# Two graph layers on one core: first weights behind the apply, and other places for biases, loads and norm parts

## The chip, the cores and the metric

The kernel runs on one core of a Trainium2 chip. A core has five engines, each with its own instruction stream: TensorE (PE, matrix multiplication, with weight loads as a second row PEld), VectorE (DVE), ScalarE (ACT), GpSimd (POOL) and SyncE (SP). SP, ACT and POOL also start DMA transfers, each through a queue of its own. Matmul results land in PSUM and are read from there by DVE or ACT.

The metric is the device time of one launch in microseconds. Six runs of the kernel before gave a median of 1492.16 us, between 1490.14 and 1496.52.

## The reference

`x` has 8 batches, 2048 nodes and 64 features; `adj` is a 2048 x 2048 matrix. Two layers follow each other. Both apply a polynomial of the graph, with weights of their own for each node, made from an embedding of 16 numbers per node:

```python
# layer 0: supports I, A, 2*A@A - I
w = einsum('nd,dkio->nkio', embedding, weight);  b = einsum('nd,do->no', embedding, bias)
out = einsum('bnki,nkio->bno', einsum('knm,bmc->bnkc', A_stack, x), w) + b
x = layernorm(x + out)
# layer 1: the same three supports of adj, and a fourth
apt = softmax(relu(E @ E.T), axis=1)
x = layernorm(x + out_of_four_supports)
```

## The kernel before

The nodes are cut into 8 blocks of 256 (`NBLK`, `NB`), two slabs of 128 each. There are 40 stages, 8 for each of five phases, numbered n = 8 * phase + j:

- A0: u = A x of layer 0, and for block j the part of the output that comes from x and u (stages 0 to 7)
- B0: A u, the third support, and the layer norm (8 to 15)
- A1: the same as A0 for layer 1, and row maxima and sums for the softmax (16 to 23)
- Z1: the softmax matrix times x (24 to 31)
- V1: A u for layer 1, the last weights, the norm and the output (32 to 39)

Each stage has one large product on PE (`straight`, `strassen`, `turned`). Most products are done by a Strassen scheme of seven products, named p1 to p7; a product goes to one of two PSUM accumulators (`ps_acc`, two buffers), and DVE or ACT adds it up elsewhere before that accumulator can be used again.

Between the matmuls of the product other work is put by hand: `put(n, i, f, ...)` says that `f` is emitted in stage n when i of 64 parts of its product are done; `spread` puts a list of jobs at even distances. So the order on each engine is written out in the lines 738 to 843, and all engines execute in that order. The jobs that matter here:

- `weights(g0, g1)` (line 313): makes groups of the weights of a block, `pw` = embedding times weight pool, four matmuls each, into a PSUM buffer of the pool `big` (three buffers); `copy` evicts it into `w`, on DVE (even first argument) or on ACT. The 16 groups of a block are cut into six bursts (`cuts`). `w_room` is one buffer: all weights of a block are used before those of the next are written.
- `apply(c)` (line 334): `po` = features times weights, 64 small matmuls in four calls; each call takes one `big` buffer, and DVE adds it to `acc` in four instructions. In stages A0, A1 and V1 all four calls stand at one place (`bursts`).
- `bias` (line 301): `pb`, then two DVE additions into `bx`, which POOL stores in DRAM; `load_acc` reads it back as the first value of `acc`.
- `post(k)` (line 363): after the apply. With k = 0 it stores `acc` (A0, A1), or starts the norm: mean and squares (0), the sum of the squares and the root (1), the multiplication and the store (2).
- `load_e` loads the embedding of a block (`e2`, two buffers), and for Z1 the softmax constants `c`.
- `load_x` reads the normed x of a block back (`x1d`) as a slab of `X` for layer 1.
- `repeat(s)` (line 569): in B0 a half of the features `t` has to stand in both halves of the partitions, so it is copied by a DMA (`t<-t`).
- `wst` and `adj` (class `Ahead`): SP's loads of weight pools and adjacency tiles, a few tiles ahead.

The last B0 stage (j = 7) has its own places, since layer 1's first product, in stage 16, already reads x:

```python
bursts, posts = (6, 6, 12, 12), ()
put(n + 1, 26, st.load_x, range(SB))
for k in range(6):
    put(n + 1, (13 if k < 3 else 14) + 2 * k, st.post, k % 3, 8 - k // 3 * 8, 16 - k // 3 * 8)
```

Of the kernel before, what the change touches and what calls it, by code (L numbers as in the profile page):

```python
# [23 lines left out]
NBLK = N // NB  # L24
SB = NB // P
# [4 lines left out]
V1 = C // 4  # L30
# [18 lines left out]
def two_graph_layers(ctx: ExitStack, tc: tile.TileContext, x, x_t, adj_b, adj_q, layers, out):  # L49
# [21 lines left out]
    pe, dve, act, pool = (Pinned(tc, e) for e in (nc.tensor, nc.vector, nc.scalar, nc.gpsimd))  # L71
# [18 lines left out]
    def big(name):  # L90
        return ps_big.tile([P, 2, 512], F32, tag="big", name=name)

    def copy(i, dst, src):

        if i % 2:
            act.activation(dst, src, AF.Copy)
        else:
            dve.tensor_copy(dst, src)
# [42 lines left out]
    ps = big("pi")  # L141
# [120 lines left out]
    class Stage:  # L262
# [50 lines left out]
        def weights(self, g0, g1):  # L313
            if g0 == 0:
                self.w = w_room[:, 0:NB * self.units].rearrange("p (n o) -> p n o", n=NB)
            made = []
            for g in range(g0, g1):
                if g % 4 == 0:
                    self.ws = wst.next()
                ps = big("pw").rearrange("p h (v n) -> p h v n", n=NB)  # L320
                for i in range(2):
                    for h in range(2):
                        r = slice(64 * h, 64 * h + 64)
                        pe.matmul(ps[:, h, i, :], self.ws[r, 2 * (g % 4) + i, :], self.e2[r, :],
                                  start=True, stop=True)
                made.append(ps)
            if g1 == self.units // 4:
                wst.fill()
            for g, ps in zip(range(g0, g1), made):
                dst = self.w[:, :, 4 * g:4 * g + 4].rearrange("p n (v h) -> p n v h", h=2)  # L330
                copy(0 if g % (8 if self.phase == "A0" else 3) == 1 else 1, dst, ps.rearrange("p h v n -> p n v h"))


        def apply(self, c):
# [234 lines left out]
        def repeat(self, s):  # L569

            if self.wide:
                self.pair[s].store_z()
            if self.half:
                t = self.t[:, s * P:(s + 1) * P, :]
                pool.dma_start(out=t[64:128, :, :], in_=t[0:64, :, :])

        def turned(self, stationary, moving):

# [133 lines left out]
    sums = {}  # L712
# [27 lines left out]
    def put(n, i, f, *args):  # L740
        plans[n].setdefault(i * stages[n].length / 64, []).append((f, args))

    def spread(n, first, last, jobs):
        for i, job in enumerate(jobs):
            put(n, first + (last - first) * i / max(len(jobs) - 1, 1), *job)
# [20 lines left out]
        put(1, place, sums["A0"].make, i)  # L766
    put(8, 2, load_u, (NBLK - 1,))
    for i in range(4):
        put(16, 24 + 4 * i, sums["A1"].make, i, 0, 7)
        put(16, 50, sums["A1"].make, i, 7, 8)  # L770
    for i, place in ((0, 10), (2, 20), (3, 30)):
        put(32, place, sums["V1"].make, i)
# [1 line left out]
    for n, st in enumerate(stages):  # L774
        phase = st.phase
        cuts = (0, 3, 6, 9, 12, 14, 16) if st.units == C else (0, 3, 6, 8)
        weights = [(st.weights, *g) for g in zip(cuts, cuts[1:])]
        bursts = None
        if phase == "A0":
            for c in range(NJ // 4 if st.j == 1 else 0):  # L780
                put(n, 16 * c + 10, st.sums_of_a, c)
            spread(n + 1, 1, 31, weights)
            turned, bursts, posts = 33, (38, 38, 38, 38), (50,)
        elif phase == "B0":
            if st.j == 7:
                spread(n, 40, 60, weights)
                bursts, posts = (6, 6, 12, 12), ()
                put(n + 1, 26, st.load_x, range(SB))
                for k in range(6):
                    put(n + 1, (13 if k < 3 else 14) + 2 * k, st.post, k % 3, 8 - k // 3 * 8, 16 - k // 3 * 8)  # L790
            else:
                spread(n + 1, 3, 13, weights)
                bursts, posts = (19, 19, 29, 29), (38, 42, 48)
                put(n + 2, 5, st.load_x, range(SB))
        elif phase == "A1":
            spread(n + 1, 12, 36, weights)
            turned, bursts, posts = 4, (43, 43, 43, 43), (56,)
            for s, h, place in ((0, 0, 38), (0, 1, 40), (1, 0, 57), (1, 1, 60)):
                put(n, place, st.scores_of_rows, s, h)
            put(n, 41, st.statistics, 0)  # L800
            put(*((n, 62) if st.j else (n + 1, 6)), st.statistics, 1)
            put(n + 1, 24, st.store_c)
        elif phase == "V1":
            spread(n, (22 if st.j else 4), (62 if st.j < 7 else 52), weights)
            bursts, posts = (4, 4, 4, 4), (15, 19, 23)
            put(n, 20, st.load_z)
        if bursts and n + 1 < len(stages):
            if phase[0] == "A":
                put(n + 1, turned, st.turn, 1)
            for i, place in enumerate(bursts):  # L810
                put(n + 1, place, st.apply, i if phase == "A0" else i ^ 2)
            for k, place in enumerate(posts):
                put(n + 1, place, st.post, k)
        if n + 1 < len(stages):
            if n < 25 or n > 30:
                put(n, 44 if n < 23 else 37 if n < 25 else 4, stages[n + 1].load_e)
        if phase[0] == "A":
            put(*((1, 12) if n == 0 else (n, 28) if st.li == 0 else (n, 37)), st.bias)
            if st.li == 0:
                put(max(n, 1), 20 if n else 4, st.load_xt)  # L820
            else:
                put(n, 47 if st.j else 57, st.turn, 0, "x")
        if phase != "Z1":
            put(*((1, 26) if n == 0 else (n, 48 + 6 * st.li) if st.kk == 0 else (n, 30)), st.load_acc)
        elif st.wide:
            first, even, odd = (n - 2, (16, 24, 32), (40, 48, 56)) if n % 2 == 0 else (n - 2, (28, 36, 44), (4, 12, 20))
            load = (n - 2, 4) if n % 2 == 0 else (n - 3, 20)
            if n == 26:
                first, even, odd, load = 25, (4, 10, 18), (20, 26, 34), (24, 40)
            elif n == 27:  # L830
                first, even, odd, load = 25, (56, 61, 67), (42, 48, 54), (25, 33)
            put(*load, st.load_e)
            for t, places in enumerate((even, odd)):
                for i, place in enumerate(places):
                    at = (first, place) if place < 64 else (first + 1, place - 64)
                    put(*at, *((st.numerators, t, i) if i < 2 else (st.normalize, t)))
        else:
            st.p = [None] * 8
            for c in range(8):
                if c < 3:  # L840
                    put(n - 1, (50, 54, 62)[c] if n < 26 else 40 + 8 * c, st.scores, c)
                else:
                    put(n, 8 * (c - 3), st.scores, c)
# [71 lines left out]
```

## Time and profile before

| what | us |
|---|---|
| median of six runs | 1492.16 |
| the profiled execution | 1492.26 |
| its span on the core | 1490.5 |
| PE busy | 1452.7 |
| DVE busy | 954.1 |
| ACT busy | 473.8 |
| POOL busy | 206.7 |

The page cuts the span into 40 slices of 37 us. A digit is the busy share in tenths:

```profile
PE   9899999999999999899999999999999999999996
DVE  3876666637666666766666666568794466666665
ACT  1344444432211213064444444432110233333332
PEclk9999999999999999999999999999999999999998
DMA  9788898884666666578877887212313656666551
```

The first nine slices are A0, the next seven or so B0, then A1 from about 600 us, Z1 from about 930 us and V1 from about 1165 us to the end. PE is busy nearly always, so the engines beside it matter where PE waits for them. A PE that is busy is not a PE that works without loss: switches between kinds of matmuls, and a slower clock, count as busy.

The costliest groups of the page are these (busy us in total, mean ns of one, idle time before and what ended it):

```profile
L43 ACT ACTIVATE w<-pw 128x1024 f32<-128x1024 f32 x328 | 318.4, 1021 | 392.7 <-PE pw L43 388.1
L43 DVE SCALAR_TENSOR_TENSOR acc<-po,mask,acc 128x256 f32<-128x256 f32 (+1 forms) x640 | 247.0, 426 | 83.2 <-PE po L43 70.4
L43 DVE COPY w<-pw 128x1024 f32<-128x1024 f32 x120 | 146.9, 1224 | 141.7 <-PE pw L43 140.4
```

All operations go through one helper, so every line is L43, and one has to go by the names of the tiles.

### The profile page before, as it was taken

To read this page: it belongs to the slowest core of one execution; us is meant where nothing else is said; L and a number is where in the kernel's file an instruction comes from. 1 tells how busy PE (TensorE), PEld (TensorE's weight loads), DVE (VectorE), ACT (ScalarE), POOL (GpSimd) and SP (SyncE) were. 2 spreads that over 40 slices of the span, in tenths; PEclk is the share of its full clock that TensorE was granted. 3 is DMA by queue.
4 is the path that set the end of the run, shared out by engine and by line. 5 is a ranking of instruction groups with operands and counts; after the bars stand their busy time and mean duration, and the time that the engine had idled before them with its cause. 6 is when DMAs were issued, how large, how long until landed. Compare 5 with 4: busy or idle time off the path is not lost.

```text
span 1490.5 us, 31130 instructions
## 1 busy us (share of the span) xinstructions
PE 1452.7 (97%) x13310; PEld 1183.2 (79%) x13310; DVE 954.1 (64%) x1614; ACT 473.8 (32%) x590; POOL 206.7 (14%) x343
## 2 busy tenths in 40 slices
PE   9899999999999999899999999999999999999996
PEld 4467777778999999468777777788888888888885
DVE  3876666637666666766666666568794466666665
ACT  1344444432211213064444444432110233333332
POOL 4222221210111111111011111101100000000100
PEclk9999999999999999999999999999999999999998
DMA  9788898884666666578877887212313656666551
GB/s 361 250 281 263 276 280 266 271 314 156 203 191 200 203 203 206 146 172 183 201 195 169 207 210 207 52 40 65 91 43 115 203 180 194 190 190 192 192 192 54
DMA packets 86730, 283.37 MB, mean 190 GB/s; under 512 B 14016, under 2 KB 18112, under 8 KB 84992
## 3 DMA queue, kind: packets, MB, share of 16 engines
q1 hardware_dynamic: 53600, 171.99, 39.6%
q0 software_dynamic: 27520, 95.76, 21.0%
q10 hardware_dynamic: 5472, 13.63, 2.8%
q8 instruction: 105, 1.72, 0.5%
q14 instruction: 33, 0.27, 0.1%
HBM read 216.28 MB, written 60.83 MB: 186 GB/s over the span
## 4 chain that ended last, share of the span: by engine, by line
PE 70%; issue 20%; DVE 3%; DMA 3%; POOL 3%; ACT 1%; POOLq 0%; ACTq 0%; DVEq 0%
PE p L43 40%; PE po L43 11%; PE pw L43 8%; PE pz L43 6%; PE pu L43 2%; PE pt L43 1%; DMA x<-in_x 1%; DVE w L43 1%; PE pr L43 1%; DVE acc L43 1%; PE ps L43 1%; POOL e L43 1%; POOL x1d L43 1%; DMA u<-in_w 1%; DMA wst<-wd 1%
## 5 line engine op out<-in xcount | busy, mean ns | idle before, releaser
L43 ACT ACTIVATE w<-pw 128x1024 f32<-128x1024 f32 x328 | 318.4, 1021 | 392.7 <-PE pw L43 388.1
L43 DVE SCALAR_TENSOR_TENSOR acc<-po,mask,acc 128x256 f32<-128x256 f32 (+1 forms) x640 | 247.0, 426 | 83.2 <-PE po L43 70.4
L43 DVE COPY w<-pw 128x1024 f32<-128x1024 f32 x120 | 146.9, 1224 | 141.7 <-PE pw L43 140.4
L43 PE MATMUL p<-a,u 128*128 128x128 f32 x1792 | 219.7, 278 | 4.1 <-PE p L43 3.9
L43 PEld LDWEIGHTS p<-a,u 128*128 128x128 f32 x1792 | 206.7, 192 | 15.1 <-issue 5.0
L43 PE MATMUL po<-w,t 128*32 128x256 f32 (+1 forms) x5120 | 205.8, 337 | 6.0 <-issue 3.1
L43 PE MATMUL p<-u,a 128*128 128x256 f32 x832 | 203.6, 387 | 0.0
L43 PEld LDWEIGHTS po<-w,t 128*32 128x32 f32 (+1 forms) x5120 | 125.9, 108 | 79.6 <-issue 12.0
L43 PEld LDWEIGHTS p<-u,a 128*128 128x128 f32 x832 | 152.1, 190 | 29.7 <-issue 5.4
L43 PE MATMUL p<-x,a 128*128 128x256 f32 x624 | 152.6, 385 | 0.0
L43 PE MATMUL pw<-e,wst 64*128 64x256 f32 x1728 | 146.1, 297 | 1.6 <-ACT w L43 1.1
L43 PEld LDWEIGHTS pw<-e,wst 64*128 64x128 f32 x1728 | 112.2, 184 | 42.3 <-issue 21.5
L43 PEld LDWEIGHTS p<-x,a 128*128 128x128 f32 x624 | 114.3, 190 | 18.9 <-issue 0.7
L43 PE MATMUL pu<-x,a 128*128 128x512 f32 x192 | 91.9, 626 | 2.8 <-DMA x<-x1d 2.6
L43 PE MATMUL p<-w,u 128*128 128x256 f32 x384 | 85.8, 379 | 0.0
L43 PE MATMUL p<-a,x 128*128 128x128 f32 x672 | 83.1, 278 | 0.1
L43 PE MATMUL p<-a,w 128*128 128x128 f32 x672 | 81.3, 277 | 0.0
L43 PEld LDWEIGHTS p<-a,x 128*128 128x128 f32 x672 | 77.8, 192 | 3.0 <-issue 0.2
L43 PEld LDWEIGHTS p<-w,u 128*128 128x128 f32 x384 | 72.1, 190 | 9.3
L43 PEld LDWEIGHTS p<-a,w 128*128 128x128 f32 x672 | 77.3, 192 | 2.5 <-issue 1.4
L43 PEld LDWEIGHTS pu<-x,a 128*128 128x128 f32 x192 | 36.6, 198 | 45.3 <-issue 38.1
L43 DVE TENSOR_TENSOR temps<-p,temps 128x256 f32<-128x256 f32 x108 | 43.1, 420 | 44.4 <-PE p L43 43.7
(122 smaller groups left out, 1412.4 us busy)
## 6 DMA issues: line engine op xcount, KB each, us to landing
wst<-wd SPq DMA_DIRECT2D x108, 512.0 KB, 6.7
a<-in_adj_q SPq DMA_DIRECT2D x87, 512.0 KB, 5.4
a<-sd SPq DMA_DIRECT2D x84, 512.0 KB, 4.2
sd<-a POOLq DMA_DIRECT2D x24, 512.0 KB, 6.5
a<-in_adj_b SPq DMA_DIRECT2D x16, 512.0 KB, 6.6
bx<-bx POOLq DMA_DIRECT2D x32, 256.0 KB, 7.1
acc<-bx POOLq DMA_DIRECT2D x16, 512.0 KB, 6.1
pd<-acc POOLq DMA_DIRECT2D x16, 512.0 KB, 5.3
```

The costliest lines, as they stand in the source:

```text
L43: return self._tc.keep_in_program_order(f(*args, **kwargs))
```

## The change

The last t copy (block 7, both halves) is issued on ACT's queue in place of POOL's. In the stages of A0, A1 and V1 with j over 0, the first group of weights is made right behind the apply of the block before, in the stage before the one where the others follow for A0 and A1, and in the same stage for V1; the other fifteen groups go in five bursts of three. Stage 0's weights are all evicted by ACT; in the other A0 stages the two groups that DVE evicts are 2 and 10 in place of 1 and 9. The other edits are places: the biases of A0 (28 to 36; stage 0's from place 12 of stage 1 to 48 of stage 0) and A1 (37 to 38.5), the last two norm parts of B0 (42 and 48 to 46.5 and 50), the applies, norm parts and x load of the last B0 block, sums for layer 1 two places earlier, `load_acc` of A0 from 48 to 54, and the loads of e and c for stages 28 to 31 earlier.

```diff
-                copy(0 if g % (8 if self.phase == "A0" else 3) == 1 else 1, dst, ps.rearrange("p h v n -> p n v h"))
+                copy(0 if self.n and g % (8 if self.phase == "A0" else 3) == (2 if self.phase == "A0" else 1) else 1, dst, ps.rearrange("p h v n -> p n v h"))
...
-                pool.dma_start(out=t[64:128, :, :], in_=t[0:64, :, :])
+                (act if self.j == NBLK - 1 else pool).dma_start(out=t[64:128, :, :], in_=t[0:64, :, :])
...
-        put(16, 24 + 4 * i, sums["A1"].make, i, 0, 7)
+        put(16, 22 + 4 * i, sums["A1"].make, i, 0, 7)
...
         cuts = (0, 3, 6, 9, 12, 14, 16) if st.units == C else (0, 3, 6, 8)
+        behind = {"A0": 38, "A1": 43, "V1": 4}.get(phase) if st.j else None
+        if behind:
+            put(n, behind, st.weights, 0, 1)
+            cuts = (1, 4, 7, 10, 13, 16)
...
-                bursts, posts = (6, 6, 12, 12), ()
-                put(n + 1, 26, st.load_x, range(SB))
+                bursts, posts = (2, 2, 10, 10), ()
+                put(n + 1, 18, st.load_x, range(SB))
                 for k in range(6):
-                    put(n + 1, (13 if k < 3 else 14) + 2 * k, st.post, k % 3, 8 - k // 3 * 8, 16 - k // 3 * 8)
+                    put(n + 1, (11 if k < 3 else 12.5) + 0.5 * k, st.post, k % 3, 8 - k // 3 * 8, 16 - k // 3 * 8)
...
-                bursts, posts = (19, 19, 29, 29), (38, 42, 48)
+                bursts, posts = (19, 19, 29, 29), (38, 46.5, 50)
...
-            spread(n + 1, 12, 36, weights)
+            spread(n + 1, 12, 34.5, weights)
...
-            put(*((1, 12) if n == 0 else (n, 28) if st.li == 0 else (n, 37)), st.bias)
+            put(n, 48 if n == 0 else 36 if st.li == 0 else 38.5, st.bias)
...
-            put(*((1, 26) if n == 0 else (n, 48 + 6 * st.li) if st.kk == 0 else (n, 30)), st.load_acc)
+            put(*((1, 26) if n == 0 else (n, 54) if st.kk == 0 else (n, 30)), st.load_acc)
...
-            load = (n - 2, 4) if n % 2 == 0 else (n - 3, 20)
+            load = ((25, 40) if n == 28 else (n - 3, 4)) if n % 2 == 0 else (n - 3, 8)
```

## The prediction

> **What bounds the kernel.** I read the page first. TensorE (PE) is busy 1452.7 of 1490.5 us, VectorE (DVE) 954.1, ScalarE (ACT) 473.8. A PE that is 97% busy leaves the change two things to win: PE's idle gaps, and work that PE repeats because it is switched between kinds of matmul. So I read next what PE waited for (columns: who waited, for whom, us in total, times, longest):
>
> ```profile
> PE p L43 <- PE p L43: 3.9, 6, 0.7
> PE ps L43 <- DMA e<-ed: 3.9, 2, 2.1
> PE po L43 <- issue: 3.1, 5, 0.9
> PE po L43 <- DMA t<-t: 2.8, 1, 2.8
> PE pu L43 <- DMA x<-x1d: 2.6, 1, 2.6
> PE pw L43 <- DVE bx L43: 2.4, 1, 2.4
> PE pw L43 <- DVE w L43: 1.3, 1, 1.3
> ```
>
> The sum is 20 us. Seven rows and 17 waits: each can be looked up in the timeline. The first stages of layer 0 (start us, us, what, idle before it):
>
> ```profile
> 35.72 2.84 PE L43 MATMUL pu<-x,a 128*128 128x512 f32 x6
> ...
> 40.34 0.74 PE L43 MATMUL pw<-e,wsplit 64*128 64x256 f32 x8 [1.35 <-DVE w L43]
> ...
> 47.13 0.50 PE L43 MATMUL pw<-e,wsplit 64*128 64x256 f32 x4 [2.39 <-DVE bx L43]
> 47.56 4.54 PE L43 MATMUL pu<-x,a 128*128 128x512 f32 x6
> ```
>
> Two weight bursts wait for a PSUM buffer that DVE has not emptied, and after the second wait six `pu` matmuls take 4.54 us where 2.84 is usual. The view by windows gives a granted clock of 0.62 from 47.3 to 50.7 us: a long wait is paid for twice.
>
> In stages B0 the same gap comes back six times. PE, then DVE, in one of them:
>
> ```profile
> 449.04 3.74 PE L43 MATMUL p<-a,w 128*128 128x128 f32 x32
> 453.48 5.15 PE L43 MATMUL p<-a,u 128*128 128x128 f32 x44 [0.69 <-PE p L43]
> ```
>
> ```profile
> 450.61 1.22 DVE L43 TENSOR_REDUCE dev<-sq 128x16 f32<-128x1024 f32 x1 [1.18 <-ACT sq L43]
> 451.86 0.76 DVE L43 TENSOR_TENSOR temps<-p,temps 128x256 f32<-128x256 f32 x2
> 452.53 0.84 DVE L43 TENSOR_TENSOR t<-p,temps 64x256 f32<-64x256 f32 x2
> ```
>
> The product that DVE reads at 451.86 had ended at 449.0. DVE came late because it stood 1.18 us waiting for ACT's squares and then reduced them for 1.22 us. PE's next product needs that accumulator.
>
> Between layer 0 and layer 1 (all engines):
>
> ```profile
> 594.91 0.53 POOL L43 DMA_DIRECT2D t<-t  x1 [0.86 <-DVE t L43]
> ...
> 602.73 2.01 PE L43 MATMUL po<-w,t 64*32 64x128 f32 x126 [2.80 <-DMA t<-t]
> ...
> 623.31 0.91 POOL L43 DMA_DIRECT2D x1d<-acc  x1 [4.74 <-DVE acc L43]
> ...
> 626.80 1.11 POOL L43 DMA_DIRECT2D x<-x1d  x2 [2.59 <-DMA x1d<-acc]
> ...
> 630.63 4.41 PE L43 MATMUL pu<-x,a 128*128 128x512 f32 x6 [2.64 <-DMA x<-x1d]
> ```
>
> PE waits for the copy of t, later for the last two slabs of x, and then runs slow again (4.41 for 2.84; clock 0.61). Last, what a burst of weight matmuls costs in A0:
>
> ```profile
> 170.00 0.97 PE L43 MATMUL pw<-e,wst 64*128 64x256 f32 x12
> ...
> 173.26 0.73 PE L43 MATMUL pw<-e,wst 64*128 64x256 f32 x8
> 173.92 1.13 PE L43 MATMUL p<-u,a 128*128 128x256 f32 x4
> ```
>
> From start to the next row's start, 12 take 0.90 us and 8 take 0.66: 0.06 each and 0.18 per burst. A `p` row between bursts is also about 0.2 us longer than its count times 0.2155 us, the steady step of a 128x256 pass (12 passes: 2.79 from start to start for 2.59). A burst has a fixed cost of some 0.38 us, for two switches.
>
> **What the Trainium skill says.** "TensorE: Matmul & The Clock Gate", Part 1: The HAM clock gate, has PE's clock halved after an idle window of about 3.4 us that runs freely. The trace agrees in the length of the slow stretch and in that it is partly luck, but not in the idle time needed: waits of 2.39 and 2.64 us brought it, the one of 2.80 did not. "DMA: Bandwidth & Descriptors", Queues, rings and completion order, lets each DMA engine take turns between queues, while one queue is worked in order. The trace fits: the copy of t at 594.91 stood on POOL's queue behind 512 KB of x1d<-acc (issued 592.84, landed 600.42 by its semaphore) and landed at 602.69; on a quiet queue the same copy took 2.86 us (358.43). "Perfetto Trace Analysis", Optimization Strategy, reads a gap that repeats as a want of room for the next tile: the B0 gap is that, in PSUM.
>
> **The change part by part.** The profiled execution took 1492.26 us, its span 1490.5; the median of six is 1492.16, so sums are made against 1492.2.
>
> 1. Stages 0 and 1. Of stage 0's 16 evictions of weights two leave DVE for ACT, and the bias part of stage 0 moves from stage 1 to place 48 of stage 0. Both waits (1.35, 2.39) and the slow stretch (1.70) lose their cause: 5.4 us. ACT then makes 3 copies in 2.9 us for each burst; bursts come about 3.5 us apart (three 0.86 us matmuls and 0.90), so it keeps up. The moved `pb` needs e, landed at 24.6 us, and PE gets there near 25.3; DVE adds bx (1.28) into an idle 1.96 us at 29.2. Stage 1's bias goes right ahead of the apply; the sums for `u` around it lie beside PE work.
>
> 2. B0. The reduce of the squares moves from place 42 to 46.5, behind the eviction of the product, the multiply from 48 to 50. The accumulator is free at about 451.0 instead of 453.4, ahead of PE. The next eviction is done at about 455.3, and PE wants that one at 456.2. 0.8 us each (453.48 less 449.04 plus 32 steps of 0.113), six times: 4.8.
>
> 3. Stages 15 and 16. The t copies go to ACT's queue. DVE has t ready for the first at about 595.5 (its order is 0.9 us worse there), and I give the copy 5 us beside the other traffic (2.86 quiet, 5.6 to 8.5 on POOL when busy): 600.6, 2.1 earlier. But the apply now stands at place 2, two matmuls (1.7 us) earlier, so PE waits nearly as long: gain 0.4. What counts is behind it: second apply ends at 608 for 609.4, and DVE's norm of the two halves, now in one piece ahead of the 2.02 us sums, takes 8.6 us instead of 10. x1d, x<-x1d (3.5 and 3.8) then land x at 627.7, when PE arrives. 2.9 us sooner than 630.6, plus 2.2 of slow clock, less half of a possible new slow stretch (0.9): 4.2. With the copy as slow as before it is about 2; without any wait it would be 7.
>
> 4. Z1. Embedding loads of stages 28 to 31 go ahead of the zd<-t stores on POOL that block them (16.48 us of waiting at 1012.13, the loads right behind at 1012.66). The waits are 2.05 and 1.86; I take 3.5 of 3.9, since DVE is 35 of 37 us busy soon after.
>
> 5. Weights. In 21 stages (A0, A1, V1, j over 0) six bursts become five of 12 and one of 4 behind the apply. The number of matmuls stays; in the order of the built instructions 168 separate bursts become 147 and 21 small ones. One switch of some fourteen per stage goes. No trace shows `pw` behind `po`: below, nothing is saved if that switch costs as much as two; above, all 0.38. I take 0.15: 3.2 us (0 to 8). It needs a PSUM buffer, the one of the second of the four apply tiles: DVE starts on them 2.0 us after PE (1240.35 and 1242.35 in V1) and takes 1.97 each, so it is free 1.1 us before PE is through (7.04).
>
> 6. A0's bias, place 28 to 36. `bx` (1.28 us) now stands behind the t copy and the split, right ahead of DVE's apply sums. By rows of one stage these start 1.1 us later, which eats that slack: I charge 0.15 us in six stages, 0.9. In A1 the bias moves past one `pr` only; load_acc moves behind pd<-acc on POOL and is not needed for 20 us. Nothing for both.
>
> Sum: 5.4 + 4.8 + 4.2 + 3.5 + 3.2 - 0.9 = 20.2. I leave 1.2 for short waits that were hidden by the long ones (PE's `issue` waits of 3.1 stay): 19, so 1473.
>
> **Rivals.** A, waits fill up again: the start keeps 3.0, stage 16 1.0, Z1 2.0, bursts 0.5, B0 its 4.8, less 0.9: 10.4, so 1482. For it: the DMA share is 0.8 to 0.9 in A0 and landings take 10 us near 55 us. Against: PE has no DMA wait there now. B, cheap switches: burst part 8 us instead of 3.2 and no charge in part 6: 1467. Nothing in the trace is against it but the switches themselves. C, slower: `pw` behind the apply waits for DVE, in order, with all of PE behind it, 21 times. The rest gains 17.9, so it decides from about 1.0 us a stage, that is when DVE starts its sums over 2.0 us later than now; at 1.2 us the time is 1492.2 + 25.2 - 17.9 = 1500. Against it: A1 and V1 have DVE's sums start where they did, and A0 alone moves by 1.1. D, the parts do not bite (copies of t as late, waits elsewhere): 1491.
>
> **How the numbers follow.** My forecast 0.62 (1468 to 1478), A 0.21, B 0.09, C 0.05, D 0.03. The range takes A and B in: 1466 to 1483. A measurement can tell 0.2%, 3 us: faster 0.92, same 0.03, slower 0.05.
>
> **What would show it.** Right: no PE waits for bx or w before 60 us and full clock there; no p<-p waits in B0; no `ps` wait for e; A0 stages at about 38.5 us (now 38.63); `pw` x4 behind `po` with no idle. Wrong: PE waiting for DVE acc behind the apply, a wait for t<-t over 3.5 us with a slow clock after it, or new waits for wst or adjacency tiles in stages 1 and 2.

## The result and the profile after

Nineteen runs of the changed kernel have a median of 1487.12 us (1482.61 to 1492.61), forty runs of the kernel before beside them 1493.09. The ratio is 0.9964, with a 95% interval of 0.9955 to 0.9973: 5.4 us faster (4.0 to 6.7). The forecast was 19.

The profiled execution took 1486.17 us, its span 1484.4, against 1490.5 before. What PE waited for after the change (who waited, for whom, us in total, times, longest):

```profile
PE po L43 <- issue: 5.0, 7, 1.0
PE pw L43 <- DMA wst<-wd: 4.0, 4, 1.9
PE po L43 <- DMA t<-t: 3.3, 1, 3.3
PE pt L43 <- ACT u L43: 2.6, 1, 2.6
...
PE pr L43 <- DVE sq L43: 1.0, 1, 1.0
PE ps L43 <- DVE w L43: 0.9, 1, 0.9
PE pt L43 <- DVE bx L43: 0.6, 1, 0.6
```

Every wait that the change went for is gone from this list: `p` for `p`, `ps` for e, `pu` for x1d, `pw` for bx. The rows for `wst`, `t`, u, sq, bx and `ps` are new or longer. They sum to 12.4 us (3.7 before), and they hold much of the missing gain.

Where it went can be read from the starts of the applies (`po`) on PE, taken from both traces. Each section runs from one apply to another; "forecast" is my sum, split over the same sections.

| section | before, us | after, us | change | forecast |
|---|---|---|---|---|
| start to the first apply | 63.68 | 58.73 | -4.95 | -5.4 |
| A0, to the last apply of A0 | 273.62 | 275.11 | +1.50 | -0.15 |
| B0, to the first apply of block 6 | 233.52 | 229.61 | -3.92 | -4.8 |
| passage, to the first apply of A1 (stages 15 to 17) | 95.55 | 98.78 | +3.23 | -4.2 |
| A1, to its last apply | 293.43 | 297.94 | +4.51 | -1.05 |
| Z1, to the first apply of V1 | 241.88 | 237.52 | -4.36 | -3.5 |
| V1, to the end | 288.78 | 286.71 | -2.06 | -1.05 |
| left for hidden waits | | | | +1.2 |
| sum | 1490.46 | 1484.40 | -6.05 | -18.95 |

Start, B0, Z1 and V1 came as forecast. The lines that answer to those shown of before: first the start of layer 0, then a B0 stage (PE; start us, us, idle before it at the end).

```profile
46.16 0.95 PE L43 MATMUL pw<-e,wsplit 64*128 64x256 f32 x12
47.05 2.84 PE L43 MATMUL pu<-x,a 128*128 128x512 f32 x6
...
445.06 3.74 PE L43 MATMUL p<-a,w 128*128 128x128 f32 x32
448.63 1.61 PE L43 MATMUL p<-a,u 128*128 128x128 f32 x13
```

The burst has no wait before it and the six `pu` take 2.84 us, no longer 4.54. In B0 the product follows after 3.57 us (448.63 less 445.06) where it followed after 4.44. (The view ended inside the last row, so it shows 13 of its matmuls.)

The passage between the layers, PE first and then DVE:

```profile
590.99 0.40 PE L43 MATMUL po<-w,t 64*32 64x128 f32 x2
594.70 2.72 PE L43 MATMUL po<-w,t 64*32 64x128 f32 x126 [3.31 <-DMA t<-t]
597.35 4.63 PE L43 MATMUL pu<-x,a 128*128 128x512 f32 x8
...
626.92 0.73 PE L43 MATMUL pr<-s,e 128*128 128x512 f32 x2 [1.03 <-DVE sq L43]
628.21 1.06 PE L43 MATMUL pt<-ident,x 128*128 128x128 f32 x8 [0.55 <-DVE bx L43]
...
636.78 1.97 PE L43 MATMUL pt<-ident,u 128*128 128x128 f32 x8 [2.62 <-ACT u L43]
```

```profile
623.70 2.02 DVE L43 TENSOR_TENSOR u<-u,x 128x1792 f32<-128x1792 f32 x1
625.64 1.22 DVE L43 TENSOR_SCALAR_CACHE_REDUCE sq<-pr 128x1024 f32<-128x1024 f32 x1
...
626.78 1.28 DVE L43 TENSOR_TENSOR bx<-x,pb 128x512 f32<-128x512 f32 x2
```

x landed at 622.77 and 623.56, and PE did not wait for it. But now VectorE is late: five sums of 2.02 us each, from 615.72 on, stand ahead of the square that frees PE's next `pr` buffer, and ahead of bx. In the kernel before these same sums (from 619.96) ended just as PE's wait for x did (at 630.69 and 630.63). The wait for x was hiding them. There are two slow stretches now: the granted clock was 0.50 from 595.85 to 599.26, behind the wait for `t`, and again from 636.81 to 640.22, behind the wait for u. The kernel before had one here.

### The profile page after: what moved, and what is told of

Its sections match the earlier page's. It is cut to its first block, busy times and chain, and to the rows that moved or that the text cites. A ratio compares the mean times of both kernels' runs of the same rounds, so it can differ in the third digit from the quotient of the medians.

```text
span 1484.4 us, 31154 instructions
## 1 busy us (share of the span) xinstructions
PE 1449.1 (98%) x13310; PEld 1185.7 (80%) x13310; DVE 952.9 (64%) x1612; ACT 476.8 (32%) x592; POOL 205.1 (14%) x341
## 4 chain that ended last, share of the span: by engine, by line
PE 52%; DMA 3%; issue 1%; DVE 1%; ACT 1%; ACTq 0%
PE p L43 32%; PE po L43 7%; PE pz L43 6%; PE pw L43 5%; DMA wst<-wd 3%; PE ps L43 1%; PE pt L43 1%; PE pr L43 1%; DVE acc L43 0%; ACT row L43 0%; ACT t L43 0%; ACT sq L43 0%; ACT w L43 0%; DVE t L43 0%; DVE dev L43 0%
## 5 line engine op out<-in xcount | busy, mean ns | idle before, releaser
L43 PE MATMUL pu<-x,a 128*128 128x512 f32 x192 | 88.5, 608 | 1.1 <-DMA x<-in_x 1.0
L43 ACT ACTIVATE sq<-acc 128x1024 f32<-128x1024 f32 (+2 forms) x19 | 17.5, 922 | 167.0 <-DVE acc L43 154.4
```

Of the source, the lines that this page charges most:

```text
L43: return self._tc.keep_in_program_order(f(*args, **kwargs))
```

## The experiments

Twelve more kernels were timed beside the kernel before. The text below each expectation gives the median, the ratio to the kernel before with its interval, and what the trace shows. One row of the traces is used again and again: the time of six A1 blocks, from A1's first apply to its seventh (before 248.87, changed kernel 252.71).

**A1 in six bursts** (`e1_a1_six_bursts`).

```diff
-        behind = {"A0": 38, "A1": 43, "V1": 4}.get(phase) if st.j else None
+        behind = {"A0": 38, "V1": 4}.get(phase) if st.j else None
...
-            spread(n + 1, 12, 34.5, weights)
+            spread(n + 1, 12, 36, weights)
```

> The changed kernel, but with the weights of the seven A1 blocks cut into six bursts as before (nothing behind the apply there, spread from 12 to 36). Theory W: in A1 the change brought the new waits of TensorE for the wst tile c = 3 (4.0 us in 4 waits), because the group that needs this tile now stands 2.3 parts earlier, and saved nothing in return; so all wst waits vanish and the time is 3 to 4.5 us less than the changed kernel's 1487.1, about 1483.3. Rival L: late wst tiles are luck of the DMA queues and come with either cut; TensorE still waits 3 to 4 us for wst and the time is within 1 us of the changed kernel. Rival S: the burst that was spared did save 0.15 us a stage and the waits are luck: about 1 us slower.

1483.57 us, ratio 0.9931 (0.9905 to 0.9956), six runs. The median is what theory W expected. The profiled execution is not: it was the slowest of the six (1492.51), with 7.8 us of wst waits, 3.6 of them in one. So the waits can come with the old cut too, and this run alone does not settle it.

**A1's bursts later** (`e2_a1_later`).

```diff
-            spread(n + 1, 12, 34.5, weights)
+            spread(n + 1, 12, 36, weights)
```

> The changed kernel with one number changed: in A1 the five bursts are spread from 12 to 36 in place of 34.5, so the burst that first needs wst tile c = 3 comes about 1.1 parts (0.75 us) later. Theory W (the tile is 0.6 to 2.1 us late for its place): the four waits become one or two, 1 to 1.5 us in all, and the time is 2 to 3 us less than the changed kernel's 1487.1. Rival L (luck of the queues, or the load is issued later too): waits as long as before, time within 1 us. A last burst at 36 may also stand too near to the apply at 43 for the evictions: then TensorE's wait for w before po grows by up to 0.4 us a stage, 2.8 in all.

1488.58 us, ratio 0.9964 (0.9950 to 0.9978): nothing gained. The list of waits names ScalarE's w for 4.7 us in 5 waits and wst for 1.4. Of PE's five stalls in A1 three stand under ScalarE's name and two under wst, but all five ended 0.13 to 0.14 us after a wst tile landed. A wait for several semaphores can be put down to the wrong one; here it was the tile each time. It landed 15.1 to 16.7 us after the second `ud<-u` store of the stage was issued, in the changed kernel 14.3 to 16.9. A later need did not help, since the tile came later as well.

**The passage as before** (`e3_stage16_as_before`): all five edits of the last B0 block undone (queue of the t copies, bursts, norm parts, x load, sums).

```diff
-                (act if self.j == NBLK - 1 else pool).dma_start(out=t[64:128, :, :], in_=t[0:64, :, :])
+                pool.dma_start(out=t[64:128, :, :], in_=t[0:64, :, :])
...
-        put(16, 22 + 4 * i, sums["A1"].make, i, 0, 7)
+        put(16, 24 + 4 * i, sums["A1"].make, i, 0, 7)
...
-                bursts, posts = (2, 2, 10, 10), ()
-                put(n + 1, 18, st.load_x, range(SB))
+                bursts, posts = (6, 6, 12, 12), ()
+                put(n + 1, 26, st.load_x, range(SB))
...
-                    put(n + 1, (11 if k < 3 else 12.5) + 0.5 * k, st.post, k % 3, 8 - k // 3 * 8, 16 - k // 3 * 8)
+                    put(n + 1, (13 if k < 3 else 14) + 2 * k, st.post, k % 3, 8 - k // 3 * 8, 16 - k // 3 * 8)
```

> The changed kernel with the whole block between the layers as before: t copies of the last B0 block on GpSimd's queue, applies at 6 and 12, the six norm parts at 13 to 18, the x loads at 26 and the sums for layer 1 at 24 to 36. Theory V: in the new block VectorE is the bound of stage 16 (five sums of 2.0 us stand ahead of its square for the row scores), so stage 16 lost 2.7 us against the kernel before relative to its start, while the old block kept its place; the old block in the changed kernel gives 1.5 to 3.5 us less than 1487.1, and the waits pr<-sq, pt<-bx and pt<-u in stage 16 are gone while the waits po<-t (2.8) and pu<-x (2.6) are back. Rival G: the new block is a gain of some us and the loss seen at the end of stage 16 came from elsewhere: 1 to 4 us slower than the changed kernel.

1493.20 us, ratio 0.9996 (0.9984 to 1.0008). Slower than the changed kernel: rival G, not V. The passage took 100.33 us, 1.5 more than in the changed kernel, so the new block does not cost 3 us. How much of the 1.5 it gains is not settled: the slow stretch behind the wait for `t` lasted 6.8 us here (594.85 to 601.68) and 3.4 in the changed kernel, and PE lost some 0.9 us more in it. The rest of the 6 us lies mostly in A1 (255.99 for six blocks), which the edit does not touch. But the waits tell the same story as above: with the wait for x back (2.60), the wait for u (2.18) stayed. Both bounds are there, one behind the other. The `pt` of u in the kernel before, and then the wait for x and that `pt` here:

```profile
641.76 1.09 PE L43 MATMUL pt<-ident,u 128*128 128x128 f32 x8 [0.48 <-ACT u L43]
```

```profile
626.68 2.84 PE L43 MATMUL pu<-x,a 128*128 128x512 f32 x6 [2.60 <-DMA x<-x1d]
...
637.83 1.09 PE L43 MATMUL pt<-ident,u 128*128 128x128 f32 x8 [2.18 <-ACT u L43]
```

From the end of the wait for x to the `pt` of u it is 11.13 us before (630.63 to 641.76), with the six `pu` slow at 4.41, and 11.15 here, with the same six at full clock, 2.84. So that slow stretch cost the kernel before next to nothing. VectorE works there without a gap from 619.96 to 641, and ScalarE's copy of u stands behind it; this set when the `pt` could start.

**A0's bursts earlier** (`e4_a0_earlier`).

```diff
-            spread(n + 1, 1, 31, weights)
+            spread(n + 1, 1, 29, weights)
```

> The changed kernel with one number changed: in A0 the five bursts are spread from 1 to 29 in place of 31. Theory P: the last burst has three groups where it had two, fills the three big PSUM buffers, and the transposes pt behind it wait 0.26 us a stage for ScalarE's evictions; four more matmul passes between them let the buffers come free, so a stage A0 costs 0.24 us less, six or seven times: 1.4 to 1.8 us less than the changed kernel's 1487.1, and pw to pt falls from 998 to about 740 ns plus the matmuls between. Rival Q: the 0.24 us is the price of pw standing behind po with its two switches; the stages stay as long and the time is within 0.5 us.

1492.37 us, ratio 0.9982 (0.9971 to 0.9993). The mechanism held and the time did not. The changed kernel, and below it this one, each around the last burst of a stage (PE):

```profile
171.74 0.95 PE L43 MATMUL pw<-e,wst 64*128 64x256 f32 x12
172.62 0.70 PE L43 MATMUL p<-x,a 128*128 128x256 f32 x2
173.42 1.09 PE L43 MATMUL pt<-ident,u 128*128 128x128 f32 x8
```

```profile
170.35 0.97 PE L43 MATMUL pw<-e,wst 64*128 64x256 f32 x12
171.25 1.56 PE L43 MATMUL p<-x,a 128*128 128x256 f32 x6
172.65 1.04 PE L43 MATMUL pt<-ident,u 128*128 128x128 f32 x8
```

From `pw` to `pt` the changed kernel takes 1.68 us for a burst of 0.90 and two passes of 0.2155, 0.35 too many; here it is 2.30 for the burst and six passes, 0.11 too many. Three groups fill the three `big` buffers, and `pt` waits for the first eviction (ScalarE began it at 172.34). An A0 stage fell from 38.87 to 38.55 us, less even than before (38.63). Yet the tiles of wst came late elsewhere: 1.6 us at the passage to B0, and A1 took 259.16, with a slow stretch in its first stage (44.64).

**Stores in the other order** (`e5_inv_first`).

```diff
-            for k, a in enumerate((cst, inv[:, :, 0])):
+            for k, a in ((1, inv[:, :, 0]), (0, cst)):
```

> The changed kernel with the two stores of store_c in the other order: cd<-inv first, cd<-cst behind it. In each A1 stage cd<-cst (columns of 4-byte elements) is then issued some 14 us later on GpSimd's queue. Theory S: that scattered store takes 8 to 12 us of the DMA engines and holds up what SP issues right behind it (ud<-u, an adjacency tile and the wst tile c = 3), so that this tile lands 15 to 17.5 us after the store in every kernel so far, however early it was issued; the change only moved the need to 15.2 us. Then ud<-u falls from 8-11 us to 2-4, the tile lands over 3 us earlier in the stage, the A1 waits for wst vanish and the time is 4 to 5 us less than the changed kernel's 1487.1: about 1482.5. Rival Q: SP's own queue (ud, two adjacency tiles, then wst) is the bound; the tile lands within 1 us of where it did and the time is within 1 us.

1483.53 us, ratio 0.9936 (0.9921 to 0.9950), 3.6 us under the changed kernel; the two intervals do not touch. `cd<-cst` is 1 KB, 256 elements of 4 bytes. The transfers issued from 722 to 734 us, in the changed kernel (first) and here (issues, KB each, median us from issue to landing):

```profile
DMA packets 471, 1.10 MB, mean 92 GB/s; under 512 B 75, under 2 KB 75, under 8 KB 471
...
q1 hardware_dynamic: 439, 1.10, 84.6%
...
ud<-u SPq DMA_DIRECT2D x2, 256.0 KB, 8.1
...
wst<-wd SPq DMA_DIRECT2D x1, 512.0 KB, 9.8
cd<-cst POOLq DMA_DIRECT2D x1, 1.0 KB, 10.8
```

```profile
DMA packets 900, 2.72 MB, mean 226 GB/s; under 512 B 109, under 2 KB 109, under 8 KB 900
...
q1 hardware_dynamic: 900, 2.72, 66.8%
...
ud<-u SPq DMA_DIRECT2D x2, 256.0 KB, 2.4
...
wst<-wd SPq DMA_DIRECT2D x1, 512.0 KB, 3.4
```

The row `q1` gives the packets, MB and share of the 16 DMA engines' time of the queue that holds SP's transfers. With the 1 KB store in flight it moved 92 GB/s, without it 226; and yet the engines were more busy with it: 439 packets took 84.6% of their time, 900 took 66.8%. In six stages the tile took 9.2 to 11.5 us in the changed kernel and 3.4 to 4.5 here, with the same place in the queue. PE at that tile, changed kernel and then this one:

```profile
738.25 0.51 PE L43 MATMUL pw<-e,wst 64*128 64x256 f32 x4 [0.42 <-DMA wst<-wd]
```

```profile
737.04 0.97 PE L43 MATMUL pw<-e,wst 64*128 64x256 f32 x12
```

No A1 wait for wst is left and six blocks take 248.37. Theory S holds. The store comes 14 us later, beside the other small store of its stage, and collides there with tiles that nobody waits for.

**Row scores early** (`e6_scores_early`).

```diff
-            for s, h, place in ((0, 0, 38), (0, 1, 40), (1, 0, 57), (1, 1, 60)):
+            for s, h, place in ((0, 0, 38 if st.j else 20), (0, 1, 40 if st.j else 21), (1, 0, 57), (1, 1, 60)):
...
-            put(n, 41, st.statistics, 0)
+            put(n, 41 if st.j else 21, st.statistics, 0)
```

> The changed kernel with the first row scores and statistics of stage 16 at places 20 and 21 in place of 38, 40 and 41, ahead of the five 2.02 us sums on VectorE. Theory V: in the new block between the layers VectorE, and behind it ScalarE's table load and two exponentials, set when PE goes on: pr waits for sq (1.03), pt for bx (0.55), pt for u (2.62). With the squares ahead of the sums these three go, except up to 1.2 for bx; PE then meets the last slabs of x (landed 622.8 to 623.6) with at most 1 us of wait. 2.5 to 4 us less than the changed kernel's 1487.1. Rival X: x is as late as VectorE, and a wait for x<-x1d of 2 us or more takes the place: within 1.5 us of 1487.1.

1490.13 us, ratio 0.9976 (0.9966 to 0.9985). The passage took 97.84 us, 0.9 less, not 2.5 to 4: sq no longer holds PE, but the next `pr` waits 1.7 for bx, and u is as late (2.4). The sums were only moved back, and all that stood behind them with them. The median is 3 us above the changed kernel's and stays unexplained: the profiled execution was the fastest of 22 and six A1 blocks in it took 252.89.

**A0 in six bursts** (`e7_a0_six_bursts`).

```diff
-        behind = {"A0": 38, "A1": 43, "V1": 4}.get(phase) if st.j else None
+        behind = {"A1": 43, "V1": 4}.get(phase) if st.j else None
```

> The changed kernel without the group behind the apply in A0 alone: six bursts (0,3,6,9,12,14,16) from place 1 to 31, as before. Theory P: the burst behind the apply saves no more than it costs and the last burst of three makes pt wait, so A0 stages go back from 38.86 to 38.63 or a little less from apply to apply; 1.4 to 1.8 us less than the changed kernel over six stages, plus the wait at the passage to B0 (wst, 0.3 us in the profile) if it comes from the bursts. Rival B: bias and load_acc in their new places cost the 0.23; the stages stay at 38.86 and the time is within 0.5 us of 1487.1.

1487.63 us, ratio 0.9964 (0.9952 to 0.9976). A stage takes 38.72 us: 0.15 less than the changed kernel, 0.09 more than before. With `e4_a0_earlier` this splits A0. The other edits of A0 (bias, `load_acc`, DVE's two groups) cost 0.09 a stage together; no run splits them. The group behind the apply saves 0.17 (38.72 to 38.55) when `pt` finds a buffer, and costs 0.15 when it does not. The time did not follow; in the profiled execution six A1 blocks took 256.40, with a slow stretch in the first (44.59).

**All three** (`e8_three`): the edits of e5, e6 and e7.

> The three edits together: stores of store_c in the other order, row scores of stage 16 early, A0 in six bursts. If the three causes are separate and each is as measured alone, the gains add: some 4.5 + 3.3 + 1.6 = 9.4 us less than the changed kernel, about 1478, and nearly what my forecast of 1473 left out. If they share a cause (one wait hides another), the sum falls short by 3 us or more.

1480.66 us, ratio 0.9919 (0.9905 to 0.9932): 6.5 us less than the changed kernel, 2.9 short of the sum. Most of the shortfall is the passage: 97.40 us, a gain of 1.4 for the 3.3 expected; e5 alone had brought 0.9 less than I counted. A1 takes 248.44.

**VectorE relieved in stage 16** (`e9_stage16_relieved`): on top of the edits of e5 and e7,

```diff
-                put(n, place, st.scores_of_rows, s, h)
-            put(n, 41, st.statistics, 0)
-            put(*((n, 62) if st.j else (n + 1, 6)), st.statistics, 1)
+                put(*((n, place) if st.j else (n + s, (0.5, 8)[s] + h)), st.scores_of_rows, s, h)
+            put(n, 41 if st.j else 1.5, st.statistics, 0)
+            put(*((n, 62) if st.j else (n + 1, 10)), st.statistics, 1)
...
-            put(n, 48 if n == 0 else 36 if st.li == 0 else 38.5, st.bias)
+            put(n, 48 if n == 0 else 36 if st.li == 0 else 38.5 if st.j else 1.7, st.bias)
```

> Stores of store_c swapped and A0 in six bursts as in e8_three; in stage 16 the first row scores, their statistics and the bias now stand at places 0.5 to 1.7, ahead of the apply, where TensorE and VectorE wait for the copy of t anyway, and the second row scores and statistics go to stage 17 (places 8 to 10). Theory V (VectorE bounds stage 16; in e8_three PE still waits 1.66 for bx and 2.40 for u, because bx and the t copy stand behind five sums): the waits for sq, bx and u all go, and PE's matmuls for pr and pb fill some 2.5 of the 3.3 us that it waits for t; from the first apply to the one of stage 16 (before 95.6, changed kernel 98.8, e8_three 97.4) it takes 92 to 94 us: 1475 to 1477.5, 3 to 5 less than e8_three. Rival X: x<-x1d becomes the bound as soon as VectorE is not; a wait for it of 2 us or more appears and the time stays within 1.5 us of e8_three's 1480.7.

1480.43 us, ratio 0.9918 (0.9905 to 0.9932): the rival. The waits for bx and u went, the one for sq moved ahead of the apply (0.73), and PE waited 1.14 for t in place of 3.31, with full clock behind it. In their place (PE):

```profile
594.72 3.70 PE L43 MATMUL pu<-x,a 128*128 128x512 f32 x8
...
620.99 2.86 PE L43 MATMUL pu<-x,a 128*128 128x512 f32 x6 [2.39 <-DMA x<-x1d]
...
640.18 1.70 PE L43 MATMUL pw<-e,wst 64*128 64x256 f32 x8 [2.17 <-ACT w L43]
641.81 3.78 PE L43 MATMUL p<-u,a 128*128 128x256 f32 x8
```

x is late again, and the scores that I moved into stage 17 put ScalarE's exponentials among the evictions of weights; after that wait eight passes take 3.78 us for 1.99. The passage: 97.02.

**The norm between the applies, and A0 as in e4** (`e10_best`): as e9, with one half of the norm earlier, and A0's group behind the apply for blocks 1 to 6 with bursts to place 29.

```diff
-        behind = {"A1": 43, "V1": 4}.get(phase) if st.j else None
+        behind = {"A0": 38, "A1": 43, "V1": 4}.get(phase) if st.j and n != 7 else None
...
-                    put(n + 1, (11 if k < 3 else 12.5) + 0.5 * k, st.post, k % 3, 8 - k // 3 * 8, 16 - k // 3 * 8)
+                    put(n + 1, (3 if k < 3 else 12.5) + 0.5 * k, st.post, k % 3, 8 - k // 3 * 8, 16 - k // 3 * 8)
...
-            spread(n + 1, 1, 31, weights)
+            spread(n + 1, 1, 29 if behind else 31, weights)
```

> As e9_stage16_relieved, and in addition the first half of the last norm stands between the two applies of stage 16 (x lands about 1.2 us sooner), and A0 has its first group behind the apply again for blocks 1 to 6, with the five bursts spread only to place 29 so that pt finds a free buffer. In e4_a0_earlier an A0 stage took 38.57 us from apply to apply, in e7_a0_six_bursts 38.72, in the changed kernel 38.86. Theory P: the group behind the apply saves 0.15 us a stage once pt does not wait: 0.8 us over six stages less than e9_stage16_relieved, and 0 to 1 from the norm. Rival: wst tiles come late somewhere in A0 or at the passage to B0 and eat it: no faster than e9_stage16_relieved.

1476.85 us, ratio 0.9894 (0.9878 to 0.9911), 3.6 less than e9, more than the 0.8 to 1.8 expected. The traces show 0.8 in five A0 stages (38.56 each), 0.9 in the passage, where the wait for x is gone; about 2 us is in neither, and the spread of executions may hold it.

**The kernel before with the stores swapped** (`e11_before_inv_first`): the diff of e5, on the kernel before.

> The kernel before with nothing changed but the order of the two stores in store_c. Theory S: the scattered store makes the wst tile land 15 to 17 us after it there too, but the kernel before needs it only 16.8 us after; so the profile shows the tile landing over 3 us earlier, and the time changes by less than 1 to 2 us (only the executions in which the tile was late gain). Rival: the store costs the kernel before as much as the changed one by other ways (adjacency tiles, ud): 3.5 us faster, as e5_inv_first against the changed kernel.

1492.44 us, ratio 1.0004 (0.9992 to 1.0016). In six stages the tile landed 10.8 to 11.6 us after the second `ud<-u` store where it had landed 13.7 to 16.4, and nothing came of it: six A1 blocks took 249.07. The store disturbed before as well (the tile took 6.0 to 8.7 us, and 3.1 to 3.9 here), but the kernel before needs the tile later: its trace has one wait of 0.39 for it.

**Scores ahead of the turn** (`e12_scores_before_turn`): as e10, with

```diff
-                put(*((n, place) if st.j else (n + s, (0.5, 8)[s] + h)), st.scores_of_rows, s, h)
+                put(*((n, place) if st.j else (n + s, 0.5 + h)), st.scores_of_rows, s, h)
...
-            put(*((n, 62) if st.j else (n + 1, 10)), st.statistics, 1)
+            put(*((n, 62) if st.j else (n + 1, 3)), st.statistics, 1)
```

> As e10_best, but the second row scores and statistics of block 0 stand at places 0.5 to 3 of stage 17, ahead of the turn of u, in place of 8 to 10. In e10_best ScalarE's table load and two exponentials (634.13 to 637.8) stood right among the first evictions of weights: TensorE waited 2.17 us for w and ran slow behind it (eight p matmuls in 3.78 us where 1.99 is usual). Theory A (ScalarE is the last of the bounds of this place): the exponentials end near 632, before the first eviction; wait and slow stretch go, up to 0.6 us of wait for the p1 copy may come: 2 to 4 us less than e10_best, 1473 to 1475. Rival: the t copies, now behind the exponentials on ScalarE and behind the squares on VectorE, hold the pt buffer in PSUM, and pw waits for it as long as it waited for w: within 1 us of e10_best's 1476.9.

1474.42 us, ratio 0.9883 (0.9867 to 0.9900), four runs: the fastest of all, 12.7 us under the changed kernel. Its interval overlaps that of e10, so the step from e10 to it is not settled by the times. The passage fell to 92.73 us. The wait did not go, though:

```profile
633.87 0.50 PE L43 MATMUL pw<-e,wst 64*128 64x256 f32 x4 [2.73 <-ACT w L43]
634.30 3.47 PE L43 MATMUL p<-u,a 128*128 128x256 f32 x8
```

One wait in place of the several around u and w. The exponentials ended at 631.2, as theory A had it, but the `t` copy behind them held ScalarE's first eviction of weights until 632.8, which is close to what the rival had. And the slow stretch lasted 3.4 us (634.67 to 638.08) for 6.8 in e10 (638.93 to 645.76), which is about 1 us of the 3.4 that the passage gained (an estimate from the slow rows) and is not shown to come from the edit. Theory A gave the right time by a mechanism that is only half there.

## Why the prediction was wrong

The sign was right and four of the seven sections came within about 1 us. Three failed; the misses are 7.4 us in part 3, 5.6 and 1.65 in parts 5 and 6.

**Part 1, the start: right.** 4.95 for 5.4.

**Part 2, B0: right.** 3.92 for 4.8; the stage shown gained the 0.87.

**Part 3, the passage: wrong, and the largest miss.** The step that failed is "2.9 us sooner than 630.6, plus 2.2 of slow clock", counted as gain.

The 2.9 first. Counted from the start of the passage, x landed after 59.32 us. It had landed after 59.77 before, and the forecast was 56.9. So x came 0.4 us sooner, and PE had no wait for it because PE was late as well. Two terms ahead of it were too small: t landed at 594.65, 6.4 us after its issue, where I gave it 5, and the slow stretch that I counted at half came in full: `po` x126 2.72 for 2.01 and `pu` x8 4.63 for 3.70, 1.64 us together. (The apply moved ahead of four `pu` matmuls, not two; the 1.7 us for them is right.)

Then the 2.2. I had asked what ended the wait in the kernel before and not what ended second. By e3 (11.15 us from x to the `pt` of u at full clock, 11.13 before with slow clock) the slow clock behind x cost nothing: VectorE's row of sums, squares and bias and ScalarE's copy of u behind it were ready no sooner. And the change made this row later within its stage: from the first apply of the last B0 block to the `pt` of u it took 45.79 us for 42.23, of which 1.71 is the earlier place of that apply. The wait of 2.62 for u then brought the second slow stretch (`pt` 1.97 for 1.09, `p` x8 2.73 for 1.89, 1.7 us). e6 and e8 (squares gone, bx and u still late) and e9 (the waits for bx and u gone, x late again by 2.39) show the layers one by one.

The Trainium skill ("TensorE: Matmul & The Clock Gate", Part 1: The HAM clock gate) has the clock halved after an idle window of about 3.4 us. The wait of 3.31 comes near that, and the slow stretches last 3.4 us or twice that. But waits of 1.51 (A1's first stage in e4 and e7), 2.17 (e9) and 2.73 (e12) brought slow stretches as well, and one of 2.40 for u in e8 did not: the measurement decides, as before. Of the new block's parts only the sum is measured, at most some 1.5 us in the passage (e3).

**Part 4, Z1: right.** 4.36 for 3.5.

**Part 5, bursts: the size was right, the place of the loss was missed.** I took 0.15 us a block; with nothing in the way the blocks gained 0.19 in V1 (38.37 to 38.18), 0.17 in A0 (e7 against e4) and 0.21 in A1 (41.39 to 41.18 in the undisturbed stages of e9, e10 and e12). (My count of 168 bursts was off: the trace has 126 in these 21 stages, and 105 with 21 small ones after. The saving for each stage does not rest on it.) What I did not work out is that fewer, larger bursts move the groups inside a stage: group 12 stood first in the fifth burst at place 31.2 and stands third in the fourth at 28.9, about 1.4 us sooner by the trace (it was needed 16.1 us after the second `ud<-u` store, and now 14.5 to 14.8). The tile for it landed 13.7 to 16.4 us after that store before, and 14.3 to 16.9 after. So the six blocks took 3.84 us more, most of the 4.5 that section A1 lost where I had minus 1.05. The other 0.67 is in its last block (45.23 for 44.56). There a burst of three fills the `big` buffers right ahead of `ps`, which waits 0.85 us for VectorE's eviction (949.13). That block takes 45.2 to 45.3 in every kernel with the new cut in A1 and 44.5 to 44.6 with the old one (before, e1, e11); no run tried it alone. I had named "new waits for wst or adjacency tiles in stages 1 and 2" as a sign of being wrong, and looked for them in the wrong phase. That the store `cd<-cst` makes the tile late is shown by e5; with e11 beside it, that it costs only where the tile is needed soon. The clearest sight of it is the row of six A1 blocks: 252.7 to 259.2 us in the six kernels with the new places and the old order of stores (the changed kernel, e2, e3, e4, e6, e7; in e4 and e7 a slow stretch adds to it), 247.2 to 248.4 in the five with the new order (e5, e8, e9, e10, e12). e1, with the old cut, stands with the first group by its profiled execution (257.56) and with the second by its median; how often the tile is late with that cut stays open.

**Part 6, A0: half right.** I charged 0.15 a stage for the bias; by e7 all the other edits of A0 together cost 0.09. That the last burst would fill PSUM right ahead of `pt` is what part 5 and part 6 both lacked: I had checked that a buffer is free for the group behind the apply, not for what follows the burst that grew. It cost 0.32 a stage (38.87 to 38.55).

**The rivals.** A, waits that fill up again, had the mechanism in two places and 1482; I gave it 1.0 us of gain in stage 16 and 0.5 in the bursts where both became losses. B and C did not come: `pw` x4 behind `po` does not wait for VectorE (669.27, at once behind an apply that began at 662.23).

## What to carry to other kernels

When a wait is to be removed, write down for that place when each of the other engines and transfers would have been ready, and count as gain only the way to the second. When work is cut into other pieces, list what every piece needs (tiles, PSUM buffers) and when it now needs it, not only the cost of the pieces. A queue that lands late and in a bunch need not have too much to move: look for one small, scattered transfer in flight beside it before moving loads about.

## What was not expected of the hardware

A store of 1 KB in 256 elements of 4 bytes took 8 to 13 us, and with it in flight there came only 92 GB/s of SP's transfers of 256 and 512 KB, against 226 without it (e5). By the two `q1` rows, a packet of these transfers held an engine some 2.6 times as long (an estimate: 84.6% for 439 packets, 66.8% for 900). The Trainium skill ("DMA: Bandwidth & Descriptors", Why small descriptors are slow (HBM only)) gives a fixed cost of some 3 cycles for each packet and 32 bytes of metadata for each operation. By that, as an estimate, 256 elements add 8 KB, which would hardly be seen beside 512 KB. The trace of the stage shown has 2.6 to 3.9 times the latency of e5 for the five transfers of SP that were issued in the 6 us behind the store. By what way it blocks them was not tried, nor whether the number of elements is what matters.

Single executions of one kernel differ by 11 us here (e6: 1484.98 to 1496.05), and A1 alone by several between kernels that do not differ in A1. A profile of one execution shows which wait is there, and not how often.
